# Order of work in a two-layer transformer kernel: routing, expert tiles, shared expert and norms at other places

## The chip, the cores and the metric

The kernel runs as one program on one core of a Trainium2 chip. The core has TensorE (PE, whose weight loads are shown apart as PEld), VectorE (DVE), ScalarE (ACT), GpSimd (POOL), and SyncE (SP), which here only issues DMAs. Every engine takes its own instructions in order. The metric is device time in microseconds: the median of the runs. Beside it stands one execution under the profiler, with its own time.

## The reference, cut to what matters

The input x has 8 sequences of 256 tokens with 128 channels, 2048 tokens in all. All is float32.

```python
xn = layernorm(x)
x  = x + attn0(xn) + ffn0(xn)
xn = layernorm(x)
x  = x + attn1(xn) + ffn1(xn)
# attn0: 16 heads of 8 channels, softmax over all 256 keys, output projection with bias
# ffn0:  8 experts (2 x 176 up, silu(gate)*up, 176 down); the two best of softmax(x @ gate_w.T),
#        weighted by their softmax values; plus sigmoid(x @ sg.T) * shared expert (352 wide)
# attn1: 8 query heads of 128 over one key/value head, causal, sine positions added to q and k
# ffn1:  8 experts (512 wide, gelu, biases b1 and b2); the best one of
#        softmax((x @ wg_red.T) @ unit_rows(wg).T), times its softmax value
```

Layernorm has no weights: (x - mean) / sqrt(var + 1e-5).

## The kernel before, in words

Tokens lie in 16 tiles of 128 on the partitions. `acc` (128 x 16 x 128) holds the running sum x, and every part of a layer is added into it. `xT` holds the normalised tokens, transposed. `layernorm(layer, blk)` works on blocks of four tiles: statistics on DVE (L237, L238), the square root on ACT (L240), its reciprocal and the normalised `xn` on DVE (L242, L246), four transposes on PE (L254), a copy to `xT` (L255), and a DMA of `xn` to DRAM (`xd`, L256), from which experts gather their tokens.

**Layer 0.** After four norms, the values (L448) and the router's softmax (`l0_router`), `l0_project(0)` makes queries and keys of two sequences (L466). Then the first scores of sequence 0 are computed for their maxima (L623, reduced by DVE at L638). The main loop has 64 steps, eight for each of the 8 sequences. A step computes two heads' scores of the next sequence for the maxima (L623, L638) and the same heads' scores of this one with the maxima already added (L666), which ACT turns into exponentials (L678); every second step multiplies these with the values (L693), normalises (L707 to L710) and, once a sequence, projects (L722) and adds to `acc` (L726). The scores use two PSUM tiles of two banks each (`big`); everything else has three single banks (`bank`) and one `held`.

At the end of each step `between(step)` puts in other work. In steps 0 to 10 it takes two pieces a step from `routing("l0")`, a generator: it ranks the tokens of each expert and makes the list of tokens for 40 expert tiles of 128 places (L306 to L413; the list comes from matmuls of comparison masks, L400). When it is exhausted, the first gather of tokens (`slot_tokens`, an indirect DMA on POOL, L417) and the first nine tiles' weights (`l0_weights`, on SP) are issued. From step 11 (`FIRST`) on, each step has one expert tile: its tokens are turned (`l0_turn`, L528, L530), then up matmuls (L536), silu as tanh on ACT (L544) with two DVE operations (L545, L547), then, a step later, down matmuls (L555), a copy (L564), the next weights, and after each four tiles a store of the results to DRAM (`put_results`, L435). After the last tile `l0_back` gathers the results of eight token tiles, two gathers each, and from step 59 (`COMBINE`) on `l0_combine` adds them, weighted, to one tile of `acc` a step (L579), and issues the gathers for a tile eight further.

After the loop a section works block by block: the shared expert (`shared_up`, L781, with ACT's Silu at L789 and a product at L790; `shared_down`, L797, added to `acc` at L807), the remaining sums of L579, the second `layernorm`, and layer 1's values and router logits (L847). Then follow the router (`l1_router`), the whole of `routing("l1")` for 24 expert tiles, and the biases of each tile's expert (`l1_biases`, L887 to L898).

**Layer 1.** `l1_project` (L991) makes queries and keys of two sequences at a time. Each sequence has four units (`l1_probs`, `l1_pv`): scores (L1016), the mask (L1024), maximum (L1026), exponentials with their sums (L1032), division (L1043), transposes (L1052), the product with the values (L1059) and, after four units, the projection (L1070) with one more small matmul for the experts' bias b2 weighted by the router (L1077; its operand is turned in `l1_scores_down`, L872, L880). The exponentials of a unit and the products of the one before it stand next to each other. After four sequences come the 24 expert tiles in six groups (`l1_group`: L916, L936, Gelu L945, L923, copy L956, store L435), with a ring of five weight slots filled by SP (L907, L908); then the results are gathered and added in the last two sequences (L1121).

What sets the order: the program's text gives each instruction a priority, and the tile framework's planner places instructions on each engine by its own estimate of when they are ready. So an instruction can run earlier than its place in the text: the first operation of `l1_gate_weights` (L814) stands after the loop in the text and runs at 14.17 us. Once placed, an engine's order is fixed, and an instruction that waits holds all behind it.

Of the kernel before, what the change touches and what calls it, by code (L numbers as in the profile page):

```python
# [10 lines left out]
F32 = mybir.dt.float32  # L11
# [5 lines left out]
P = 128  # L17
# [8 lines left out]
NG = 4  # L26
# [17 lines left out]
YT = 8  # L44
EPS_LN = 1e-5
# [5 lines left out]
def two_layer_kernel(  # L51
# [56 lines left out]
    eps_ln = ctile([P, 1], "eps_ln")  # L108
    nc.gpsimd.memset(eps_ln, EPS_LN)
# [72 lines left out]
    b2_s = ctile([NE, E], "b2_s")  # L182
# [7 lines left out]
    nc.gpsimd.dma_start(b2_s, b2)  # L190
# [23 lines left out]
    wqp = ctile([P, H0, ROW], "wqp", wp)  # L214
    wkp = ctile([P, H0, ROW], "wkp", wp)
# [15 lines left out]
    def layernorm(layer, blk):  # L231
# [7 lines left out]
        sd = small.tile([P, TPB], F32, tag="ln_sd", name=f"sd_{nm}")  # L239
        nc.scalar.activation(sd, mv[:, :, 1], AF.Sqrt, bias=eps_ln)  # L240
        rs = small.tile([P, TPB], F32, tag="ln_rs", name=f"rs_{nm}")
        nc.vector.reciprocal(rs, sd)  # L242
# [247 lines left out]

    ws0 = ctile([P, NTILE], "ws0")
# [30 lines left out]

    def l0_turn(i):
        g, t = divmod(i, GRP)
        if t == 0 and g + 1 < NS0 // GRP:
            xs0[g + 1] = slot_tokens(0, g + 1, r0)
        ps = bank(f"xg0_{i}")
        nc.tensor.transpose(ps[:, :P], xs0[g][:, t, :], ident)  # L528
        xg0[i] = work.tile([P, P], F32, tag="wtT", name=f"xg0_{i}")
        nc.scalar.copy(xg0[i], ps[:, :P])  # L530

    def l0_up(i):

        ps = bank(f"u0_{i}")
        for c in range(4):
# [8 lines left out]
        nc.scalar.activation(sg, ps[:IC, : 2 * P], AF.Tanh, scale=0.5)  # L544
        nc.vector.scalar_tensor_tensor(sg, sg, 1.0, ps[:IC, : 2 * P], ALU.add, ALU.mult)  # L545
        h0[i] = work.tile([IC, 2, P], F32, tag="h1", name=f"h0_{i}", bufs=3)
        nc.vector.scalar_tensor_tensor(  # L547
            h0[i].rearrange("p c n -> p (c n)"), sg, 0.5, ps[:IC, 2 * P :], ALU.mult, ALU.mult
# [36 lines left out]
    FIRST = 11  # L585
    COMBINE = FIRST + NS0 + 8

    def between(step):

        if step < FIRST:  # L590
            for _ in range(2):
                if next(routing0, routing0) is not routing0:
                    continue
                if not xs0:
                    xs0[0] = slot_tokens(0, 0, r0)
                    for i in range(RING0):
                        l0_weights(i)
        i = step - FIRST
# [9 lines left out]
        if step >= COMBINE and step - COMBINE < NTILE:  # L608
            l0_combine(step - COMBINE)
# [120 lines left out]
    for i in range(0, NI, 2):  # L730
        pair = [big_tile(f"s1_0_{i + h}") for h in range(2)]
        issue(*(max_scores(0, i + h, pair[h]) for h in range(2)))
        for h in range(2):
            max_rows(0, i + h, pair[h])

# [40 lines left out]
    def shared_up(blk):  # L776
        h = work.tile([P, len(CH), BLK], F32, tag="c", name=f"hs_{blk}")
        for c, n in enumerate(CH):
            ps = big_tile(f"sh_{blk}_{c}")
            for k in range(2):  # L780
                nc.tensor.matmul(  # L781
                    ps[:n, ts(k, BLK)],
                    lhsT=shu_s[:, k, ds(P * c, n)],
                    rhs=xT[:, ts(blk, BLK)],
                    start=True,
                    stop=True,
                )
            sg = work.tile([P, BLK], F32, tag="e", name=f"sg_{blk}_{c}", bufs=4)
            nc.scalar.activation(sg[:n, :], ps[:n, :BLK], AF.Silu)  # L789
            nc.vector.tensor_tensor(h[:n, c, :], ps[:n, BLK:], sg[:n, :], ALU.mult)  # L790
        return h

    def shared_down(blk, h):
        ps = bank(f"ds_{blk}")
        for t in range(TPB):
            for c, n in enumerate(CH):
                nc.tensor.matmul(  # L797
                    ps[:, ts(t, P)],
                    lhsT=h[:n, c, ts(t, P)],
                    rhs=shd_s[:n, c, :],  # L800
                    start=(c == 0),
                    stop=(c == len(CH) - 1),
                )
        for t in range(TPB):
            n = blk * TPB + t
            a = acc[:, n, :]
            nc.vector.scalar_tensor_tensor(  # L807
                a, ps[:, ts(t, P)], ws0[:, n : n + 1], a, ALU.mult, ALU.add
            )


    def l1_gate_weights():
        sq = small.tile([NE, 16], F32, tag="wg_sq", name="wg_sq")
        nc.vector.tensor_tensor(sq, wg_s, wg_s, ALU.mult)  # L814
        n2 = small.tile([NE, 1], F32, tag="wg_n2", name="wg_n2")
        nc.vector.tensor_reduce(n2, sq, AX.X, ALU.add)
        n1 = small.tile([NE, 1], F32, tag="wg_n1", name="wg_n1")
        nc.scalar.activation(n1, n2, AF.Sqrt)
        nc.vector.tensor_scalar_max(n1, n1, EPS_WG)
        rn = small.tile([NE, 1], F32, tag="wg_rn", name="wg_rn")  # L820
        nc.vector.reciprocal(rn, n1)
        unit = small.tile([NE, 16], F32, tag="wg_u", name="wg_u")
        nc.vector.tensor_scalar(unit, wg_s, rn, None, ALU.mult)
        ps = bank("wgT")
        nc.tensor.matmul(
            ps[:16, :NE], lhsT=unit, rhs=ident[:NE, :NE], start=True, stop=True
        )
        unitT = small.tile([16, NE], F32, tag="wg_uT", name="wg_uT")
        nc.vector.tensor_copy(unitT, ps[:16, :NE])
# [132 lines left out]
    for blk in range(NBLK + 1):  # L962
        h = shared_up(blk) if blk < NBLK else None
        if blk > 0:
            shared_down(blk - 1, late)
            for t in range((blk - 1) * TPB, blk * TPB):
                if t >= 2 * NI * NG - COMBINE:
                    l0_combine(t)
# [247 lines left out]
```

## Time and profile before

| | |
|---|---|
| runs | 674.85, 679.87, 681.44 us; median 679.87 |
| profiled execution | 677.03 us, of which the span of instructions is 675.3 |
| busy PE, PEld, DVE, ACT, POOL | 562.2, 391.7, 399.7, 261.5, 127.2 us |
| mean granted TensorE clock | 0.919 of full |
| instructions | 10890 |
| DMA | 42.20 MB, mean 62 GB/s |

Times count from the first instruction. In a timeline line the columns are start, duration (of a run of equal instructions: to its end), engine, line, operation, output <- inputs, count, and in brackets the idle time before it with what ended it. "issue" is time that an engine spent on no wait the profile shows. Busy time of PE is modelled and overlaps, so 90% busy is not 90% of what PE could do. The granted clock tells which share of full speed PE's clock had.

### The profile page before, as it was taken

To read this page: it belongs to the slowest core of one execution; us is meant where nothing else is said; L and a number is where in the kernel's file an instruction comes from. 1 tells how busy PE (TensorE), PEld (TensorE's weight loads), DVE (VectorE), ACT (ScalarE), POOL (GpSimd) and SP (SyncE) were. 2 spreads that over 40 slices of the span, in tenths; PEclk is the share of its full clock that TensorE was granted. 3 is DMA by queue.
4 is the path that set the end of the run, shared out by engine and by line. 5 is a ranking of instruction groups with operands and counts; after the bars stand their busy time and mean duration, and the time that the engine had idled before them with its cause. 6 is when DMAs were issued, how large, how long until landed. Compare 5 with 4: busy or idle time off the path is not lost.

```text
span 675.3 us, 10890 instructions
## 1 busy us (share of the span) xinstructions
PE 562.2 (83%) x3860; PEld 391.7 (58%) x3860; DVE 399.7 (59%) x942; ACT 261.5 (39%) x667; POOL 127.2 (19%) x157
## 2 busy tenths in 40 slices
PE   3879799999999998489862688897899989589786
PEld 2544566576757775145452555565668987456564
DVE  6575786667666776425647585667573324376753
ACT  2302134444544444143511024415339994141532
POOL 7100015033213201760300130000013304400000
PEclk9977799999999999799976598898899999699799
DMA  8100313144424510110100510000008972100000
GB/s 229 36 1 0 107 48 96 55 113 121 116 54 120 91 32 22 51 48 1 45 26 16 159 27 1 2 0 1 0 14 255 235 232 60 51 9 7 2 8 9
DMA packets 49863, 42.20 MB, mean 62 GB/s; under 512 B 4728, under 2 KB 44736, under 8 KB 49808
## 3 DMA queue, kind: packets, MB, share of 16 engines
q1 hardware_dynamic: 45248, 33.52, 17.2%
q0 software_dynamic: 3984, 7.71, 5.3%
q8 instruction: 31, 0.51, 0.3%
q10 hardware_dynamic: 576, 0.27, 0.2%
q14 instruction: 24, 0.20, 0.1%
HBM read 34.14 MB, written 7.34 MB: 61 GB/s over the span
## 4 chain that ended last, share of the span: by engine, by line
PE 57%; issue 16%; DVE 12%; ACT 7%; DMA 5%; POOL 1%; SPq 0%; POOLq 0%; DVEq 0%; ACTq 0%
PE s L1016 6%; PE s L623 6%; PE o L1059 5%; PE u L536 4%; PE qk L991 4%; PE wo L1070 4%; PE d L555 3%; ACT p L1032 3%; PE pv L693 3%; PE pT L1052 3%; PE d L923 2%; PE u L936 2%; PE qk L466 2%; PE s L666 2%; PE sh L781 2%
## 5 line engine op out<-in xcount | busy, mean ns | idle before, releaser
L417 POOL DMA_INDIRECT xs<-xd,d_ids_l x64 | 63.9, 999 | 342.7 <-DVE d_ids_l L413 121.9
L678 ACT ACTIVATE eT<-s 128x1024 f32<-128x1024 f32 x64 | 65.2, 1024 | 113.8 <-PE s L666 113.8
L623 PE MATMUL s<-qk 32*128 32x256 f32 x512 | 81.2, 443 | 23.0 <-DVE mx L638 22.8
L638 DVE TENSOR_REDUCE mx<-s 128x4 f32<-128x1024 f32 x64 | 77.6, 1218 | 23.4 <-PE s L666 17.0
L1016 PE MATMUL s<-kT,qT 128*128 128x128 f32 (+1 forms) x256 | 58.8, 364 | 22.5 <-ACT p L1032 22.5
L623 PEld LDWEIGHTS s<-qk 32*128 32x128 f32 x512 | 48.0, 204 | 47.5 <-DVE mx L638 30.0
L666 PE MATMUL s<-qa,qk 32*128 32x256 f32 x512 | 72.8, 416 | 2.2 <-ACT eT L678 1.2
L1032 ACT ACTIVATE p<-s,ms 128x128 f32<-128x128 f32 (+1 forms) x128 | 52.2, 428 | 41.4 <-PE s L1016 33.7
L417 POOL DMA_INDIRECT yt<-yg,d_pos_l x48 | 48.1, 1001 | 105.8 <-issue 46.9
L1016 PEld LDWEIGHTS s<-kT,qT 128*128 128x128 f32 x256 | 41.8, 206 | 37.9 <-ACT p L1032 30.6
L1059 PE MATMUL o<-pT,v 128*128 128x512 f32 x96 | 50.2, 634 | 8.3 <-DVE ms L1028 4.8
L1062 ACT COPY oT<-o 128x512 f32<-128x512 f32 x32 | 18.9, 590 | 82.3 <-PE o L1059 82.3
L666 PEld LDWEIGHTS s<-qa,qk 32*128 32x128 f32 x512 | 43.8, 192 | 8.4 <-issue 3.5
L693 PE MATMUL pv<-eT,va 128*32 128x256 f32 x512 | 42.0, 401 | 1.2 <-ACT eT L678 1.2
L536 PE MATMUL u<-xg,gu_s 128*88 128x128 f32 x320 | 41.6, 273 | 0.0
L536 PEld LDWEIGHTS u<-xg,gu_s 128*88 128x88 f32 x320 | 37.0, 157 | 0.3 <-issue 0.3
L1070 PEld LDWEIGHTS wo<-wo_s,oT 128*128 128x128 f32 x256 | 32.0, 195 | 5.2 <-issue 4.2
L1052 PE MATMUL pT<-ident,p 128*128 128x128 f32 x192 | 32.6, 312 | 2.3 <-DVE p L1043 1.3
L1070 PE MATMUL wo<-wo_s,oT 128*128 128x128 f32 x256 | 34.1, 282 | 0.0
L1043 DVE TENSOR_SCALAR p<-p,rec 128x128 f32<-128x128 f32 (+1 forms) x128 | 32.5, 317 | 1.0
L1024 DVE TENSOR_TENSOR s<-s,mask 128x512 f32<-128x512 f32 x32 | 22.3, 696 | 18.2 <-PE s L1016 18.1
L1052 PEld LDWEIGHTS pT<-ident,p 128*128 128x128 f32 x192 | 27.6, 164 | 9.1 <-DVE p L1043 2.9
(219 smaller groups left out, 945.0 us busy)
## 6 DMA issues: line engine op xcount, KB each, us to landing
w_up<-in_w_dram SPq DMA_DIRECT2D x30, 256.0 KB
gu_s<-in_gu_dram SPq DMA_DIRECT2D x40, 176.0 KB
w_down<-in_w_dram SPq DMA_DIRECT2D x18, 256.0 KB
yg<-ys SPq DMA_DIRECT2D x16, 256.0 KB
dn_s<-in_dn_dram SPq DMA_DIRECT2D x40, 88.0 KB
xd<-xn SPq DMA_DIRECT2D x8, 256.0 KB
acc<-in_x_dram SPq DMA_DIRECT2D x4, 256.0 KB
xs<-xd,d_ids_l POOLq DMA_INDIRECT x64, 2.9
```

The source lines that it names most:

```text
L417: nc.gpsimd.indirect_dma_start(out=dst, out_offset=None, in_=table, in_offset=bass.IndirectOffsetOnAxis(ap=index, axis=0), bounds_check=ta ...
L536: nc.tensor.matmul(ps[:IC, ts(c, P)], lhsT=gu0_s[:, i % RING0, c, :], rhs=xg0.get(i), start=True, stop=True,)
L623: nc.tensor.matmul(pv[:, jj, t, :], lhsT=qT[r : r + ROW, g, ds(o + t * P, P)], rhs=kT[r : r + ROW, g, ds(o, S)], start=True, stop=True,)
L638: nc.vector.tensor_reduce(m[:, ds(2 * half, 2), :, D0 + g], pv, AX.X, ALU.max, negate=True)
L666: nc.tensor.matmul(pv[:, jj, c, :], lhsT=kT[r : r + ROW, g, ds(o + c * P, P)], rhs=qa[r : r + ROW, g, :], start=True, stop=True,)
L678: nc.scalar.activation(eT.rearrange("p j c q -> p (j c q)"), ps, AF.Exp, scale=SC0)
L693: nc.tensor.matmul(po[ds(ROW * j, ROW), ts(g % 2, S)], lhsT=va_flat[:, ds(o, ROW)], rhs=eTs[j // 2][:, j % 2, c, :], start=(c == 0), stop= ...
L1016: nc.tensor.matmul(sc[:, hh, :], lhsT=qT[:, 4 * hg + hh, ds(o + t * P, P)], rhs=kT[:, ds(o, nk)], start=True, stop=True,)
L1032: nc.scalar.activation(p[:, hh, :], sc[:, hh, :], AF.Exp, bias=ms[:, hh : hh + 1], scale=SC1, accum_out=sums[:, hh : hh + 1],)
L1052: nc.tensor.transpose(ps[:, ts(hh, P)], p[:, hh, ts(c, P)], ident)
L1059: nc.tensor.matmul(po, lhsT=v1[:, 2 * b + c, :], rhs=pT[:, c, :], start=(c == 0), stop=(c == t))
L1070: nc.tensor.matmul(ps[:, ts(t, P)], lhsT=oT[:, h, ts(t, P)], rhs=wo1_s[:, h, :], start=(h == 0), stop=False,)
```

## The change

1. `routing("l0")` is taken in pieces between the four pairs of first scores (five pieces a pair), and its rest before the loop; there the first gather, the first nine tiles' weights and the first turn are issued too. Tiles begin at step 3 (`TILES`) in place of 11. (`between` calls the turn of tile 0 in step 2 once more, with its gather of the second group.)
2. The shared expert goes into steps 44 to 59, three steps of `shared_up` (one chunk each, two single banks in place of a big tile, tanh and two DVE operations in place of Silu and one) and one of `shared_down` per block.
3. The sums of L579 go two tiles a step into steps 50 to 57.
4. The second norms of blocks 0, 1, 2 go into steps 53, 55, 59, and layer 1's first projection into steps 56 to 63; only the last norm, the values and the router follow the loop.
5. `routing("l1")` is taken one piece per unit of layer 1's attention; the first gather, first weights and biases are issued when it is exhausted.
6. 1/sqrt in `layernorm` is an add and a power (-0.5) on POOL, in place of ACT's square root and DVE's reciprocal.
7. b2 is no longer added by matmuls in the projection. Each expert tile's weights bring a third DMA, its b2 row broadcast to all partitions (`bias2`), and DVE adds it when it empties the down matmuls' bank (one per tile, in place of one copy per group from `held`). The router's weighted one-hots and their transposes go, and the score is a maximum.
8. `l1_gate_weights` stands before layer 0's router in the text.

```diff
+TILES = 3
+SHARED = TILES + NS0 + 1
+COMBINE = SHARED + 6
+NORM1 = (COMBINE + 3, COMBINE + 5, COMBINE + 9)
+PROJECT1 = COMBINE + 6
...
-        nc.scalar.activation(sd, mv[:, :, 1], AF.Sqrt, bias=eps_ln)
         rs = small.tile([P, TPB], F32, tag="ln_rs", name=f"rs_{nm}")
-        nc.vector.reciprocal(rs, sd)
+        nc.gpsimd.tensor_scalar_add(rs, mv[:, :, 1], EPS_LN)
+        nc.gpsimd.tensor_tensor(rs, rs, minus_half, ALU.pow)
...
+    def silu_times(dst, half, g, u):
+        nc.scalar.activation(half, g, AF.Tanh, scale=0.5)
+        nc.vector.scalar_tensor_tensor(half, half, 1.0, g, ALU.add, ALU.mult)
+        nc.vector.scalar_tensor_tensor(dst, half, 0.5, u, ALU.mult, ALU.mult)
...
     def between(step):
-        if step < FIRST:
-            for _ in range(2):
-                if next(routing0, routing0) is not routing0:
-                    continue
...
-        i = step - FIRST
+        i = step - TILES
...
-        if step >= COMBINE and step - COMBINE < NTILE:
-            l0_combine(step - COMBINE)
+        blk, c = divmod(step - SHARED, len(CH) + 1)
+        if 0 <= blk < NBLK:
+            if c < len(CH):
+                shared_up(blk, c)
+            else:
+                shared_down(blk)
+        if 0 <= step - COMBINE < NTILE // 2:
+            for t in range(2):
+                l0_combine(2 * (step - COMBINE) + t)
+        if step in NORM1:
+            layernorm(1, NORM1.index(step))
+        if step >= PROJECT1:
+            for _ in range(2):
+                next(project1, None)
...
             max_rows(0, i + h, pair[h])
+        for _ in range(5):
+            next(routing0, None)
+    for _ in routing0:
+        pass
+    xs0[0] = slot_tokens(0, 0, r0)
+    for i in range(RING0):
+        l0_weights(i)
+    l0_turn(0)
...
+        nc.sync.dma_start(
+            bias2[:, i % len(ring), :],
+            b2[ds(r, 1), :].rearrange("e c -> (e c)").partition_broadcast(P),
+        )
...
+            nc.vector.tensor_tensor(ys[:, t, :], pd[:, :P], bias2[:, n, :], ALU.add)
             l1_weights(g * GRP + t + len(ring))
...
+    layernorm(1, NBLK - 1)
+    for blk in range(NBLK):
+        l1_values(blk)
     oh1 = l1_router()
     r1 = Routing()
-    for _ in routing("l1", [oh1], NS1, r1):
-        pass
-    own_b1 = l1_biases(r1.expert)
+    routing1 = routing("l1", [oh1], NS1, r1)
...
                 late = (b, hg, t, p, oT)
+                if not ahead and next(routing1, routing1) is routing1:
+                    ahead.append(slot_tokens(1, 0, r1))
+                    for i in range(len(ring)):
+                        l1_weights(i)
+                    own_b1 = l1_biases(r1.expert)
```

## The prediction

> **What bounds the kernel now.** I cut the span into stages (view of busy time by stretch) at events of the timeline: first scores at 36.4, the first expert tile's matmuls (L536) at 105.1, the last tile's (L555) at 263.7, layer 1's first scores (L1016) at 395.8. Columns: start and end, length, then busy time and count on PE, PEld, DVE, ACT, POOL, then granted clock, DMA share, GB/s.
>
> ```profile
> 36.00:51.00 15.00, 10.93 (x66) 6.76 (x64) 10.84 (x19) 0.69 (x1) 0.00 (x0) 0.68 0.00 1
> 51.00:98.00 47.00, 41.61 (x302) 25.96 (x300) 33.70 (x79) 11.97 (x13) 0.21 (x1) 0.81 0.19 53
> 98.00:264.00 166.00, 159.70 (x1615) 111.54 (x1612) 113.22 (x181) 76.73 (x170) 39.78 (x40) 1.00 0.32 82
> 264.00:302.00 38.00, 23.40 (x234) 11.61 (x232) 14.15 (x27) 11.59 (x14) 25.99 (x26) 0.87 0.19 51
> 302.00:362.00 60.00, 44.17 (x208) 27.92 (x207) 32.92 (x121) 19.31 (x28) 6.11 (x6) 0.92 0.09 26
> 362.00:386.00 24.00, 11.45 (x46) 9.93 (x45) 15.78 (x62) 0.97 (x2) 0.20 (x1) 0.50 0.39 110
> 396.00:503.00 107.00, 92.82 (x432) 63.38 (x433) 71.25 (x168) 40.32 (x151) 0.18 (x1) 0.94 0.01 1
> 503.00:561.00 58.00, 54.61 (x447) 52.11 (x447) 18.76 (x37) 53.89 (x138) 15.76 (x16) 1.00 0.76 214
> ```
>
> PE sets the pace where the tiles run (159.7 of 166 us at full clock). From 264 to 386 nothing is full: PE is busy 79 of 122 us, and from 362 at half clock. The timeline shows why:
>
> ```profile
> 270.36 0.35 DVE L579 SCALAR_TENSOR_TENSOR acc<-yt,wr,acc 128x128 f32<-128x128 f32 x1 [2.31 <-DMA yt<-yg,d_pos_l]
> 275.89 0.79 PE L623 MATMUL s<-qk 32*128 32x256 f32 x2 [7.31 <-DVE mx L638]
> 320.67 1.28 ACT L240 ACT_TABLE_LOAD   x1
> 376.04 3.58 PE L400 MATMUL ids_l<-col_l,row_l 128*128 128x24 f32 x16 [7.02 <-DVE col_l L395]
> ```
>
> The sums L579 stand ahead of the maxima L638 in DVE's order and wait for gathers that Pool issues every 1.30 us, so PE waits 7.3 us. Later norms and shared expert alternate through table loads, and layer 1's routing leaves PE idle.
>
> **The change, stage by stage.** The sum is made on the profiled execution: 677.03 us, a span of 675.3 and 1.7 around it; the median of 679.87 is 2.8 above.
>
> *To 36.4: 0 (-1 to +4).* No row shows Pool's add and power on 128x4. Near rows: 0.09 us (memset 128x1), 0.14 (iota 128x16), 1.26 (tensor add 128x512). I take 0.25 each, near the small ones, against 0.30 on ACT and 0.18 on DVE now. Pool is busy with DMA issues and memsets until 11.15, so the first normalising xn goes from 9.37 to about 11.3; behind it on Pool stand the bias adds (1.26), for which DVE doesn't wait. The third block's xn already waits for the store of xn until 17.33, which covers this; without that cover it costs 2. The gate weights' square already runs at 14.17, so moving its code up is nothing.
>
> *36.4 to the first tile: -23 (-30 to -17).* Now 68.7 us. Routing costs DVE 18.8 us (59 instructions, 65.2 to 97.5) and PE eight groups of ids matmuls, 1.98 us each at full clock. The first scores use DVE for 8 x 1.22 of their 13.4 us. With both together from 39.18, ids are ready at 39.2 + 9.8 + 18.8 = 67.7 at the earliest; from ids to the first tile it is 7.8 (97.3 to 105.1: four gathers, landing, transpose), where steps 0 to 2 and the second projection fit: 75.5. The other end: eight steps fewer stand ahead of the tile, each 2.46 us without extra work (265.71 to 268.17): 105.1 - 19.7 = 85.4. I take 82, nearer to the second, since the second projection's 7 to 9 us of PE and three steps need room too. Beside it the clock: granted 0.68 there, and a group of ids matmuls takes 3.58 at 0.50. The Trainium skill (TensorE: Matmul & The Clock Gate, Part 1) says that the clock is halved after an idle window of about 3.4 us and released by sustained work. By that rule, were PE mostly waiting for DVE here, the eight groups would cost 28.6 instead of 15.8 us, and the tile would start near 88 if nothing covered it. The 0.50 row agrees with the rule.
>
> *Tiles: 0 (0 to +2).* 41 steps in 158.6 us, PE full, whatever their numbers. The first turn is called twice (ahead of the loop and in step 2): four gathers (5.2 us of Pool, busy 40 of 166), a transpose of 0.27, a copy of 0.25.
>
> *Last tile to layer 1's first scores: -32 (-42 to -6).* Now 132.2 us. What PE must do there: 12 steps of 1.9 (a batch of eight takes 28.85 with tiles at 1.7 a step) = 22.8; 8 steps without maxima of 1.65 (1.13 + 0.53) = 13.2; shared up 48 x 0.43 = 20.6; shared down 4 x 2.7 = 10.8; transposes 4 x 1.1; projection 18 x 0.43 = 7.7; values 4 x 2.2 = 8.8. Together 88. At the tiles' idle share (4%) that is 91, at that of 264 to 362 (67.6 of 98 busy) 128. I take 100, nearer to the first, since score work now stands between the shared expert's. What keeps it from 91: DVE has about 70 us here (12 x 1.22 maxima, 24 x 0.69 for silu, which is 8.3 more than with one product, 32 x 0.30 sums, 16 x 0.28, norms 3 x 3, projection 9 x 0.75, transposes). A shared chunk holds two of the three banks through two matmul pairs, tanh 0.60 and two DVE operations of 0.69, about 3.9 us, or 5.1 with a maximum between. Seven table loads go (three of L240, three of L789, one of L266), 7 x 1.28 = 9.0 us of ACT, inside this stage. The Trainium skill (ScalarE: Activation LUTs, What ACT_TABLE_LOAD costs) adds 1.38 us of drain to each, so by it 18.6 us would go. Here the activation begins at 321.96, right after the load of 320.67: no drain is seen, and 9.0 stands. Routing of layer 1 (24 us from 362) leaves this stage.
>
> *Layer 1, first half: +5 (-3 to +15).* Routing goes between 12 units of attention: 10.7 us of DVE and four groups of matmuls (7.2 at half clock, 3.6 at full), where DVE is busy 71 of 107 and PE 93. The biases' 3.7 of DVE follow. If gaps took it all it would be 0; I take a third. SP can issue the first five expert weights when the experts are known, a batch or more ahead of their use.
>
> *Experts and rest: 0 (-4 to +8).* A bias row is 128 packets more. Queue 1's 45248 packets took 17.2% of 16 x 675 us, 41 ns each: 0.33 us over 16 engines, 19 refills 6 us. The refill fills DMA for half of the stage:
>
> ```profile
> 515.00:530.00 15.00, 13.56 (x116) 13.11 (x114) 2.92 (x8) 14.74 (x42) 5.15 (x6) 1.00 0.92 263
> 530.00:545.00 15.00, 13.94 (x110) 12.99 (x109) 5.27 (x12) 14.82 (x38) 3.76 (x4) 1.00 1.04 264
> ```
>
> I take +4 of the 6. On SP a third issue is some 0.55 us on 1.7 per tile (373.62 to 375.32), below the stage's 2.4. DVE's 24 adds of 0.35 less 6 copies of 0.69 are 4.3, under DVE's 39 idle. Against it go the bias matmuls, 16 x 0.41, and the turned scores, 4 x 1.04 of PE; some 4 of these 11 lie on the path here and in the first half.
>
> Sum: -23 - 32 + 5 + 0 = -50, so 627 in the profile's terms. I say **628** for a median.
>
> **Rivals.** *The gathers hold the norms (648).* Pool is in order: the last sums' 16 gathers (20.8 us) can stand ahead of a norm's power, and DVE's xn, with the maxima behind it, waits. For: 264 to 288 lost 14 us over four steps (23.6 against 9.8). Against: seven steps of about 4 now lie between the tiles and the sums. Price: the 20.8 once, 627 + 21.
>
> *More is hidden (605).* Stage 2 at 75.5 and the fourth at 91 give 677 - 30 - 42. For: the tile stage shows that PE can be filled. Against: three banks and DVE.
>
> *Order isn't made by the program (675).* Instructions are placed by a planner: the gate's square is program-late and runs at 14.17. If the moves left the order as it is, only bias matmuls and loads count, within 1%. Against: the shared matmuls begin only at 302, behind the last scores.
>
> *Slower: one row of biases holds the experts (760).* All rows lie in one tile. If the add of a tile waited for the row last asked for, each tile would take that DMA's time; 7.55 us lies on the chain behind full queues:
>
> ```profile
> 535.78 7.55 DMA w_down<-in_w_dram
> ```
>
> 24 x (7.55 + 0.35 - 2.4) = 132 more, 759. It decides from 4.5 us a tile (2.4 + 50/24). Against: the weights are slots of one tile too, and PE waits only 0.5 us for them.
>
> **Chances.** Forecast (612 to 640) 0.55, more hidden 0.13, gathers 0.20, no change 0.04, slower 0.08. One per cent is about what a measurement of this kernel can tell from no change. Range 600 to 660: it takes in the fast rival and the gathers, and leaves out the last two. Faster 0.88, same 0.04, slower 0.08.
>
> **What will show it.** The first L536 near 82, the last L555 near 241, first L1016 near 341, first expert matmul (L936) near 452. No waits of maxima behind L579 above 3 us. No table load between 110 and the first L936. PE's clock above 0.9 in the norms. If L246 waits for Pool by more than 5 us, the gathers' rival holds; if ids are ready only after 85, the second stage is wrong; if the expert stage is over 70 us, the bias rows. What would make it wrong most: DVE as the bound of the fourth stage.

## The result, and the profile after

The changed kernel takes **647.92 us** (median of 645.86 to 651.23, four runs) against 679.54 for the kernel before beside it: a ratio of **0.955** (0.949 to 0.961). That is faster by 31.6 us, where 50 were forecast; 648 lies inside the range of 600 to 660. In the profiled execution 29.2 us of span are gone (675.3 to 646.1). The column c1 is the profiled execution of a second comparison of the same two kernels (below).

| stage, us | before | forecast change | after | c1 |
|---|---|---|---|---|
| start to first scores | 36.4 | 0 | 38.8 | 34.9 |
| first scores to first tile | 68.7 | -23 | 58.4 | 57.8 |
| 40 expert tiles | 158.4 | 0 | 158.3 | 158.4 |
| last tile to layer 1's first scores | 132.3 | -32 | 104.6 | 106.1 |
| layer 1, first half | 107.7 | +5 | 116.6 | 118.1 |
| layer 1's experts and the rest | 171.8 | 0 | 169.4 | 168.7 |

The first stage of one and the same kernel is 34.9 in one execution and 38.8 in another, so its +2.4 can't be put down to the change. A stage is read from one profiled execution of a kernel, and among the experiments below those of e8, e9 and e10 lie 12, 10 and 9 us above the fastest run of their kernel and that of e3 lies 11 us under its median, so small differences in these four say little. The forecast's gain is missing in three stages: 13 us in the second, 4 to 6 in the fourth, 4 to 5 in the fifth. Line numbers from here on are those of the changed kernel: ids matmuls L406, gathers L423, Pool's addition and power L247 and L248, `xn` L252, projection L472, turn L565, up L572, sums L613, shared up L628, shared down L643, maxima L741, layer 1's scores L1022, its experts L979 and L965.

Busy time by stretch, after the change (columns as in the prediction: start and end, length, PE, PEld, DVE, ACT, POOL, granted clock, DMA share, GB/s):

```profile
38.80:76.00 37.20, 28.61 (x141) 22.67 (x140) 26.97 (x75) 0.69 (x1) 0.00 (x0) 0.62 0.24 66
76.00:97.10 21.10, 17.55 (x92) 8.93 (x92) 6.68 (x7) 6.24 (x9) 12.15 (x12) 0.79 0.15 38
97.10:255.50 158.40, 153.48 (x1544) 107.97 (x1541) 108.17 (x174) 73.95 (x167) 31.85 (x32) 1.00 0.33 83
255.50:360.10 104.60, 83.46 (x610) 43.91 (x608) 66.19 (x155) 28.89 (x37) 36.05 (x38) 0.93 0.12 31
```

The fourth stage before the change:

```profile
263.70:395.80 132.10, 89.13 (x509) 53.70 (x508) 69.91 (x219) 32.17 (x42) 39.97 (x40) 0.82 0.18 50
```

The ids are ready at 75.7, but the first tile starts only at 97.1. The tiles' stage is as it was. The fourth stage, before at a clock of 0.82 (0.50 from 362 to 386), now runs at 0.93, and PE is busy 80% of it instead of 67%.

What lies between the ids and the first tile, in the timeline after the change:

```profile
75.50 0.20 DVE L416 TENSOR_TENSOR d_idf_l<-ids_l,d_idf_l 128x40 f32<-128x40 f32 x1 [1.51 <-PE ids_l L406]
...
79.06 0.47 PE L565 MATMUL xg<-ident,xs 128*128 128x128 f32 x1 [3.59 <-DMA xs<-xd,d_ids_l]
...
79.75 9.63 PE L472 MATMUL qk<-xT,wqkp 128*128 128x512 f32 x16
...
89.31 1.13 PE L769 MATMUL s<-qa,qk 32*128 32x256 f32 x8
...
97.15 1.11 PE L572 MATMUL u<-xg,gu_s 128*88 128x128 f32 x8
```

PE waits 3.6 us for the first gather, because the extra turn ahead of the loop is first in its queue. Then comes the second block's projection, 9.6 us, with little beside it and half of it at a granted clock of 0.50 (79.7 to 84.5; 0.95 from there to 89.4). Then come steps 0 to 2, 7.8 us. Before the change the projection took as long, 54.0 to 63.3, also with little beside it, but ahead of the routing; its first and last rows there:

```profile
54.02 1.92 PE L466 MATMUL qk<-xT,wqp 128*128 128x512 f32 x2
...
62.30 1.02 PE L466 MATMUL qk<-xT,wkp 128*128 128x512 f32 x2
```

And the longest stop in the fourth stage:

```profile
289.76 1.00 POOL L423 DMA_INDIRECT yt<-yg,d_pos_l  x1 [0.31 <-issue]
290.79 0.26 POOL L247 TENSOR_SCALAR rs<-mv 128x4 f32<-128x4 f32 x1
291.13 1.04 POOL L248 TENSOR_TENSOR rs<-rs,minus_half 128x4 f32<-128x4 f32 x1
292.21 0.60 DVE L252 TENSOR_SCALAR xn<-acc,mv,rs 128x128 f32<-128x128 f32 x2 [5.99 <-POOL rs L248]
...
293.46 2.02 PE L628 MATMUL sh<-xT,shu_s 128*96 128x512 f32 x2 [10.49 <-DVE sg L557]
```

Pool has issued 24 gathers since 259.74, one each 1.30 us, and only then comes to the addition and the power of the first norm. DVE stands at `xn` for 6.0 us (after two waits of 2.3 for sums), and behind `xn` in DVE's order stands the silu product that would free a bank for PE: PE loses 10.5 us at one wait.

### The profile page after: what moved, and what is told of

Its sections match the earlier page's. It is cut to its first block, busy times and chain, and to the rows that moved or that the text cites. A ratio compares the mean times of both kernels' runs of the same rounds, so it can differ in the third digit from the quotient of the medians.

```text
span 646.1 us, 10887 instructions
## 1 busy us (share of the span) xinstructions
PE 543.4 (84%) x3797; PEld 380.6 (59%) x3797; DVE 400.6 (62%) x959; ACT 245.1 (38%) x649; POOL 140.9 (22%) x176
## 4 chain that ended last, share of the span: by engine, by line
PE 53%; DVE 14%; issue 14%; DMA 8%; POOL 6%; ACT 5%; POOLq 0%; SPq 0%; DVEq 0%; ACTq 0%
PE s L726 6%; PE s L1022 5%; PE u L572 5%; PE o L1065 5%; PE qk L668 4%; PE qk L472 4%; PE d L589 3%; PE pv L796 3%; POOL yt L423 3%; PE pT L1058 3%; PE wo L1076 3%; ACT p L1038 3%; PE s L769 3%; PE d L965 2%; DMA yt<-yg,d_pos_l 2%
## 5 line engine op out<-in xcount | busy, mean ns | idle before, releaser
L423 POOL DMA_INDIRECT xs<-xd,d_ids_l x68 | 68.1, 1001 | 279.4 <-DVE d_ids_l L419 126.2
L741 DVE TENSOR_REDUCE mx<-s 128x4 f32<-128x1024 f32 x64 | 77.9, 1218 | 18.4 <-PE s L769 12.4
L726 PE MATMUL s<-qk 32*128 32x256 f32 x512 | 78.2, 419 | 12.7 <-DVE mx L741 12.5
L1022 PE MATMUL s<-kT,qT 128*128 128x128 f32 (+1 forms) x256 | 57.7, 362 | 20.2 <-ACT p L1038 20.2
L769 PE MATMUL s<-qa,qk 32*128 32x256 f32 x512 | 71.5, 401 | 1.1 <-DVE qa L752 0.7
L726 PEld LDWEIGHTS s<-qk 32*128 32x128 f32 x512 | 46.4, 192 | 36.0 <-DVE mx L741 20.6
L423 POOL DMA_INDIRECT yt<-yg,d_pos_l x48 | 48.1, 1002 | 79.2 <-issue 46.5
L1022 PEld LDWEIGHTS s<-kT,qT 128*128 128x128 f32 x256 | 42.1, 209 | 33.5 <-ACT p L1038 27.2
L572 PE MATMUL u<-xg,gu_s 128*88 128x128 f32 x320 | 41.6, 273 | 0.0
L796 PE MATMUL pv<-eT,va 128*32 128x256 f32 x512 | 37.3, 391 | 0.6 <-ACT eT L781 0.6
L572 PEld LDWEIGHTS u<-xg,gu_s 128*88 128x88 f32 x320 | 37.0, 157 | 0.3 <-issue 0.3
L628 PE MATMUL sh<-xT,shu_s 128*128 128x512 f32 (+1 forms) x48 | 26.8, 673 | 10.5 <-DVE sg L557 10.5
L988 ACT ACTIVATE h<-u,own_b 128x128 f32<-128x128 f32 x96 | 26.4, 379 | 20.5 <-PE u L979 20.4
L472 PE MATMUL qk<-xT,wqkp 128*128 128x512 f32 x64 | 33.6, 679 | 0.0
```

The lines of the kernel that those rows point to most:

```text
L423: nc.gpsimd.indirect_dma_start(out=dst, out_offset=None, in_=table, in_offset=bass.IndirectOffsetOnAxis(ap=index, axis=0), bounds_check=ta ...
L472: nc.tensor.matmul(ps, lhsT=w[:, ts(g, 4), :], rhs=xT[:, ts(blk, BLK)], start=True, stop=True,)
L572: nc.tensor.matmul(ps[:IC, ts(c, P)], lhsT=gu0_s[:, i % RING0, c, :], rhs=xg0.get(i), start=True, stop=True,)
L726: nc.tensor.matmul(pv[:, jj, t, :], lhsT=qT[r : r + ROW, g, ds(o + t * P, P)], rhs=kT[r : r + ROW, g, ds(o, S)], start=True, stop=True,)
L741: nc.vector.tensor_reduce(m[:, ds(2 * half, 2), :, D0 + g], pv, AX.X, ALU.max, negate=True)
L769: nc.tensor.matmul(pv[:, jj, c, :], lhsT=kT[r : r + ROW, g, ds(o + c * P, P)], rhs=qa[r : r + ROW, g, :], start=True, stop=True,)
```

## The experiments

Each comparison runs kernels and the kernel before on one chip. In the comparison of e5 to e7 and c1 the kernel before takes 677.9 us; with e1 to e4, e8 to e10 and e11 it takes 720 to 722. It isn't the chip: one chip gave 677.9 with e5 and 722.0 with e11. So ratios are compared within a level, and stages too. The changed kernel itself ran at the level of 678 only.

| stage, us | e1 | e2 | e3 | e4 | e8 | e9 | e10 | e11 | c1 | e5 | e6 | e7 |
|---|---|---|---|---|---|---|---|---|---|---|---|---|
| level of before | 720 | 720 | 720 | 720 | 720 | 720 | 720 | 722 | 678 | 678 | 678 | 678 |
| to first scores | 33.1 | 33.9 | 36.2 | 40.1 | 38.2 | 40.3 | 39.7 | 40.0 | 34.9 | 33.3 | 33.6 | 38.5 |
| to first tile | 56.1 | 55.0 | 58.0 | 57.1 | 58.3 | 54.4 | 54.4 | 54.3 | 57.8 | 53.0 | 58.3 | 58.3 |
| tiles | 165.9 | 165.8 | 165.8 | 165.9 | 167.3 | 167.8 | 167.8 | 165.9 | 158.4 | 158.4 | 158.4 | 158.4 |
| to layer 1's scores | 117.8 | 113.7 | 115.1 | 113.7 | 175.2 | 115.1 | 113.4 | 114.3 | 106.1 | 106.0 | 106.6 | 104.7 |
| first half | 118.8 | 117.1 | 111.8 | 116.2 | 102.8 | 118.9 | 119.9 | 114.8 | 118.1 | 116.5 | 123.1 | 120.2 |
| experts and rest | 173.1 | 173.1 | 176.1 | 174.6 | 175.4 | 174.8 | 175.7 | 178.7 | 168.7 | 169.5 | 172.1 | 169.3 |
| ratio | 0.928 | 0.924 | 0.939 | 0.929 | 0.991 | 0.927 | 0.926 | 0.928 | 0.952 | 0.955 | 0.970 | 0.964 |

### c1, the changed kernel again

> The changed kernel once more, on the chip of the three runs sent with it, so that their stages can be set against its own. Measured first: ratio 0.955 to before (0.949 to 0.961); stages 38.8, 58.4, 158.3, 104.6, 116.6, 169.4. If the chip is one on which before takes 720 us, the ratio should be the same, so 687 us; if it lies near 0.93 instead, the first turn and the 1/sqrt that the first four runs took away were worth nothing.

Measured: 646.10 us, ratio 0.952 (0.947 to 0.957); stages as in the first table. So the result is repeatable, and the stop of 10.49 us at L628 is there again with 10.5.

### e1, without the first turn ahead of the loop

```diff
         l0_weights(i)
-    l0_turn(0)
```

> The changed kernel without the first turn ahead of the loop; it stays in step 2 alone. Theory (the turn holds TensorE's queue): in the changed kernel TensorE waits 3.59 us for the first gather in L565, with the mask transposes and the second projection (16 matmuls, 9.6 us at half clock) behind it. Without it these start about 75.5 instead of 79.1, so the first tile goes from 97.1 to 93 or 94, and the time from 648 to about 644. Rival (the steps and the projection set the tile's start, and the gathers a wait that only moves): first tile within 1 us of 97.1, time within 1 us.

Measured: the stage is 56.1, against 58.0 and 57.1 in e3 and e4, which have the turn at the same level; ratio 0.928 (0.923 to 0.933). Of the ids' 21 us to the first tile 17.7 are left. The wait for the gather is gone and the projection starts at 70.08, beside the last ids, but three steps and most of the projection still stand ahead of the tile. The ids come 1.4 us later than in e3 and e4 (38.4 after the first scores, against 36.9 and 37.0). So the turn cost 1 to 2 us, and the larger part was what stood behind it: theory and rival each had a part.

### e2, the projection written behind the first scores

```diff
+    qa0 = l0_augment(0)
+    l0_project(1)
     for _ in routing0:
         pass
...
-    l0_turn(0)
...
```

> As the run before, and in addition the mask transposes and the second block's projection are written ahead of the last part of the routing. Theory (TensorE is idle and cold beside the routing, 28.6 of 37.2 us busy at half clock up to 76, and then does 9.6 us of projection with nothing beside it): the projection fits beside the routing, the first tile goes to 97.1 - 3.6 - 9.6 = 84, time 635 to 638. Rival (VectorE is what the routing waits for): its 4 additions of 0.75 and the 1.22 of qa delay the ids from 75.7 to 80, first tile 88 to 89, time 639 to 641. No gain at all would say that the clock or the tile's weights hold the tile.

Measured: ratio 0.924 (0.918 to 0.929), the stage 55.0. This edit didn't put the projection beside the routing: five pieces a pair use up the routing's pieces within the four pairs of first scores, so nothing of it was left behind them, and the projection ran from 70.9 to 80.5, behind the last ids matmuls. The run says only that the place behind the routing is worth 1 us. The question itself is e5's.

### e5, the projection among the first scores

```diff
             max_rows(0, i + h, pair[h])
+        if i == 2:
+            l0_project(1)
         for _ in range(5):
             next(routing0, None)
...
-    l0_turn(0)
...
-        if b % 2 == 0 and b + 2 < B:
+        if b % 2 == 0 and 0 < b and b + 2 < B:
             l0_project(b // 2 + 1)
```

> The changed kernel without the first turn ahead of the loop, and with the second block's projection written among the first scores, ahead of the routing's second group of steps. Theory (the projection is 9.6 us of matmuls that came beside the routing before the change and after it since): the stretch from the ids to the first tile goes from 21.4 to about 10 (three steps of 2.5, and the gather beside them), the ids come at most 2 us later; time 10 to 12 us less than the control, ratio about 0.938 where the control has 0.955. Rival (routing and projection need the same three banks and the same VectorE): ids 6 to 9 us later, first tile within 4 us of the control's, time 0 to 4 us less.

Measured: the ids come 40.9 after the first scores (c1: 37.0), the first tile 12.1 after the ids (c1: 20.8); the stage is 4.8 shorter, 53.0. PE in the timeline of e5:

```profile
48.58 1.05 PE L406 MATMUL ids_l<-col_l,row_l 128*128 128x40 f32 x8 [1.40 <-DVE col_l L401]
...
54.14 1.93 PE L406 MATMUL ids_l<-col_l,row_l 128*128 128x40 f32 x8
...
72.38 0.67 PE L750 MATMUL mT<-ident,mx 128*128 128x128 f32 x2
...
86.31 0.89 PE L572 MATMUL u<-xg,gu_s 128*88 128x128 f32 x6
```

Directly behind the projection a group of ids takes 1.05 us, later, when PE has gaps again, 1.93. So the projection did fit among the routing, at a price of 3.9 us for the ids: about half of what theory gave, between it and the rival. Part of the gain was lost behind the ids. With no projection there, the three steps ran at a granted clock of 0.53, though the records show PE busy throughout; in the changed kernel they took 7.8 us at 1.00:

```profile
74.40:86.30 11.90, 11.90 (x73) 6.88 (x73) 2.45 (x2) 3.23 (x4) 8.17 (x8) 0.53 0.17 44
```

The median is 644.6, ratio 0.955 (0.948 to 0.961): from the control's 646.1 this can't be told apart.

### e3 and e4, 1/sqrt on ScalarE and on VectorE

e3, as before the change:

```diff
-        nc.gpsimd.tensor_scalar_add(rs, mv[:, :, 1], EPS_LN)
-        nc.gpsimd.tensor_tensor(rs, rs, minus_half, ALU.pow)
+        nc.scalar.activation(sd, mv[:, :, 1], AF.Sqrt, bias=eps_ln)
+        nc.vector.reciprocal(rs, sd)
```

> The changed kernel with 1/sqrt as before the change: square root on ScalarE, reciprocal on VectorE. Theory (Pool's gathers hold the norms): TensorE's wait of 10.5 us at 283 and VectorE's 8.7 us for rs go, two table loads of 1.28 a norm come back on ScalarE, which is busy only 29 of the 105 us; the stage from the last tile to layer 1's first scores goes from 104.6 to between 94 and 100, the first scores from 38.8 back to 36.5, time 638 to 643. Rival (the sums wait for the gathers' data in any case, so VectorE stands as long): stage 104 to 112 with the loads, time 648 to 655.

e4, by Newton steps from a first guess on the bits:

```diff
-        nc.gpsimd.tensor_scalar_add(rs, mv[:, :, 1], EPS_LN)
-        nc.gpsimd.tensor_tensor(rs, rs, minus_half, ALU.pow)
+        nc.vector.tensor_scalar_add(va, mv[:, :, 1], EPS_LN)
+        nc.vector.tensor_scalar(rs.bitcast(I32), va.bitcast(I32), 1, None, ALU.arith_shift_right)
+        nc.vector.tensor_scalar(rs.bitcast(I32), rs.bitcast(I32), -1, 0x5F3759DF, ALU.mult, ALU.add)
+        for _ in range(3):
+            nc.vector.tensor_tensor(nw, rs, rs, ALU.mult)
+            nc.vector.scalar_tensor_tensor(nw, nw, -0.5, va, ALU.mult, ALU.mult)
+            nc.vector.scalar_tensor_tensor(rs, nw, 1.5, rs, ALU.add, ALU.mult)
```

> The changed kernel with 1/sqrt of the norms on VectorE: a shift and a subtraction on the bits for a first guess, then three Newton steps, 12 instructions on 128x4 in place of Pool's two; 12 x 0.16 = 1.9 us of VectorE a norm (estimated from 128x16 instructions of 0.17 us). Theory (Pool's gathers hold the norms): no wait for rs, stage from the last tile to layer 1's first scores 92 to 97 instead of 104.6, time 637 to 642. Rival (VectorE is the bound of that stage): 3 x 1.9 = 5.7 us more there, and the waits move to the sums: stage 104 to 110, time 648 to 654.

Measured: e3 0.939 (0.935 to 0.944; five runs from 664.7 to 678.6, median 675.5, the profiled one the lowest), e4 0.929 (0.923 to 0.935; median 670.1); the stage 115.1 and 113.7, where Pool's form gives 117.8 (e1) and 113.7 (e2) at the same level. So in the profiled executions the place of 1/sqrt moves the stage by no more than e1 and e2 differ with the same form. By the medians ScalarE's form is 5 us slower than VectorE's, with ranges that overlap; where these lie, the profile of e3, its lowest run, doesn't show. The 12 small instructions of e4 take 2.1 us a norm. The table loads that e3 brings back cost 1.28 us each on ScalarE:

```profile
304.57 1.28 ACT L248 ACT_TABLE_LOAD   x1
305.87 0.30 ACT L248 ACTIVATE sd<-mv,eps_ln 128x4 f32<-128x4 f32 x1
```

Why there is little to gain at this level is seen in e2's timeline, in the first group of the shared expert's down matmuls beside the gathers. First the same 24 matmuls in the changed kernel's own profile, then e2's first rows with Pool's:

```profile
267.74 2.94 PE L643 MATMUL ds<-shd_s,hs 128*128 128x128 f32 x24
```

```profile
267.44 0.39 PE L643 MATMUL ds<-shd_s,hs 128*128 128x128 f32 x2 [0.49 <-issue]
...
268.01 1.00 POOL L423 DMA_INDIRECT yt<-yg,d_pos_l  x1 [0.30 <-issue]
268.15 0.27 PE L643 MATMUL ds<-shd_s,hs 128*128 128x128 f32 x1 [0.32 <-issue]
...
268.87 0.99 PE L643 MATMUL ds<-shd_s,hs 128*128 128x128 f32 x4 [0.45 <-issue]
269.31 1.00 POOL L423 DMA_INDIRECT yt<-yg,d_pos_l  x1 [0.30 <-issue]
...
280.26 1.23 DVE L741 TENSOR_REDUCE mx<-s 128x4 f32<-128x1024 f32 x1 [12.57 <-PE ds L643]
```

The matmuls last to 278.9, 11.5 us in place of 2.9, and come by threes and fours while Pool issues a gather each 1.30 us; DVE waits 12.6 us. In the changed kernel's own profile Pool issues the same gathers at the same pace, and these matmuls don't stop. The same level shows it in the tiles: 165.9 in place of 158.4, with eight waits of about 2 us in e4 (DVE's silu, "issue"), each beside one of the eight groups of four gathers. So at this level other engines slow down beside gathers, whatever stands behind these in Pool's queue. And the stop that e3 and e4 were to remove is small here: PE's wait for the silu product behind `xn`, 10.5 us in the changed kernel's profile, is 2.6 in e1, with Pool's form. What makes the level isn't known.

### e9 and e11, e5 with the Newton steps

> The second projection among the first scores, no first turn ahead of the loop, and the norms' 1/sqrt by Newton steps on VectorE. Theory (24 gathers ahead of the first norm in Pool's queue cost TensorE 10.5 us at one wait): the stage from the last tile to layer 1's first scores goes from 106 to 95 to 99, ratio 0.937 to 0.943 where the projection alone gave 0.955 (0.948 to 0.961). Rival (VectorE, or the sums' own wait for gathers, holds that stage anyway, as the second chip's 113.7 by either way suggests): stage 103 to 107, ratio 0.950 to 0.956.

> The kernel of e9 once more. The chips of this study are of two kinds: on two of them the kernel before takes 678 to 680 us, on two 720, where engines stand for 12 to 17 us while Pool issues gathers, and where the norms' place made no difference. If this run falls on the first kind: theory (gathers ahead of the first norm in Pool's queue) stage from the last tile to layer 1's first scores 95 to 99 instead of 106.0, no wait for 10.5 us of the shared expert's matmuls, time 634 to 640; rival (VectorE or the sums' own wait holds the stage) 103 to 107, time 643 to 648. If it falls on the second kind: stage 113 to 116 and ratio 0.927 as in e9, and the question stays open.

Both fell on the level of 720: ratios 0.927 (0.922 to 0.932) and 0.928 (0.923 to 0.932), the stage 115.1 and 114.3. The wait for `rs` is gone, but at this level it was small (6.4 us in all in e1 and in e2), and the Newton steps of three norms take about as much on DVE. The longest wait in the stage is the one of this level, and e1 has it too, with Pool's form (waits by engine, e11 and e1; "remote" is a release the profile doesn't place):

```profile
DVE mx L752 <- remote: 13.5, 1, 13.5
```

```profile
DVE mx L741 <- PE ds L643: 13.5, 1, 13.5
```

What e11's expectation says of two kinds of chips is wrong: its chip had been at the other level before. At the level of 678, where the stop of 10.5 us stands behind Pool's queue, neither form ran, so their worth there stays **open**.

### e8, the order undone

```diff
-        blk, c = divmod(step - SHARED, len(CH) + 1)
-        if 0 <= blk < NBLK:
-            ...
-        if step in NORM1:
-            layernorm(1, NORM1.index(step))
-        if step >= PROJECT1:
-            ...
+        if step >= COMBINE and step - COMBINE < NTILE:
+            l0_combine(step - COMBINE)
...
+    for blk in range(NBLK + 1):
+        ...
```

> The changed kernel with the shared expert, the last sums, the norms, and the projections of layer 1 written behind layer 0's attention again, in the order of before; the tanh form of silu and Pool's 1/sqrt stay, so no table loads come back. Theory (the 28 us of the stage from the last tile to layer 1's first scores come from filling TensorE there): that stage goes from 105 or 106 back to 122 to 132 (132.1 before the change, up to 9 of which were table loads), time 663 to 671, ratio 0.978 to 0.99. Rival (the table loads and the serial norms were what cost): stage under 112, ratio under 0.965.

Measured: 716.1 us, ratio 0.991 (0.986 to 0.995); the stage is 175.2, against 113 to 118 in every other kernel of that level, and the first half 102.8 in place of 112 to 120. Waits in that stage of e8 (its L610 are the sums, L711 and L726 first scores and maxima, L735 the maxima's transposes, L249 and L257 `xn` and its transposes):

```profile
PE mT L735 <- DVE mx L726: 25.3, 2, 24.7
...
PE lnT L257 <- DVE xn L249: 18.4, 4, 5.8
...
DVE acc L610 <- DMA yt<-yg,d_pos_l: 17.8, 15, 2.2
DVE mx L726 <- remote: 17.4, 1, 17.4
PE s L711 <- DVE mx L726: 16.7, 7, 7.4
```

Two kinds of stop of the kernel before are among them, maxima behind sums (7.4 us the longest) and serial norms (18.4 us in four waits), and no table load is. The longest, 24.7, is for the most part the halt of this level: DVE stands 17.4 us of it at a maximum while Pool issues gathers, as it stands 12.6 to 13.5 in e1 and e2 with the new order, so 4 to 5 us of the difference may be the halt's. The rest is the order's. So it is the order that carries the fourth stage at this level; e8 undoes shared expert, sums, norms and projections together, and which of them carries how much isn't shown. Its size at this level (57 to 62 us in the stage, 41 to 51 with the first half, 48 in the medians against e1's 668.3) isn't the size at 678, where the whole stage lost 26 to 28.

### e6, the biases by matmul

```diff
-            nc.vector.tensor_tensor(ys[:, t, :], pd[:, :P], bias2[:, n, :], ALU.add)
...
+            nc.tensor.matmul(
+                ps[:, ts(t, P)],
+                lhsT=wtT[b // 2][:, ts(2 * (b % 2) + t, P)],
+                rhs=b2_s,
+                start=False,
+                stop=True,
+            )
...
```

> The changed kernel with the second biases as before the change: turned scores, and a matmul of 8 rows a tile pair in layer 1's output projection, no bias rows by DMA. Theory (rows cost the experts' stage 4 of the 6 us of their DMA time; the matmuls and turned scores cost 11 us of TensorE, about half on the path): experts' stage from 63 to 58 or 59, the rest 5 to 8 longer, time 1 to 4 us more than the control. Rival (the rows hold the experts): the experts' stage goes below 57 and the time is 3 us or more under the control's.

Measured: 656.56, ratio 0.970 (0.966 to 0.974), 10.5 us over the control. The expert stretch alone:

```profile
480.00:536.20 56.20, 52.29 (x428) 49.89 (x428) 16.81 (x32) 52.14 (x135) 15.30 (x16) 1.00 0.80 221
```

```profile
475.30:537.50 62.20, 53.88 (x435) 50.79 (x435) 21.93 (x58) 47.04 (x132) 15.16 (x16) 1.00 0.83 220
```

The first is e6, the second the control: the rows, with their additions and a bank for each tile, cost 6.0 us there. Little of this is waiting for DMA: in the control PE waits 2.1 us for weights, 3.9 for turned tokens (`xgT`, copied on DVE) and 2.3 for Gelu's result, in e6 1.5, 1.9 and 0.3. Everything after it is 9.4 shorter with rows (106.5 against 115.9), and the first half 5.0 (118.1 against 123.1). So the biases are a gain of 8 us in these stages, more than theory had, and of the other sign than the rival.

### e7, layer 1's routing written whole ahead of its attention

```diff
-    routing1 = routing("l1", [oh1], NS1, r1)
+    for _ in routing("l1", [oh1], NS1, r1):
+        pass
+    own_b1 = l1_biases(r1.expert)
...
```

> The changed kernel with layer 1's routing written whole ahead of layer 1's attention, as before the change. Theory (spread between the attention's units, the routing costs 9 us of the first half instead of 24 with TensorE waiting): first scores of layer 1 20 to 25 us later than the control's, the first half 9 us shorter (107.5 before the change), time 11 to 16 us more. Rival (the planner lays attention beside the routing anyway, as it lays the first scores beside the ids): time within 3 us of the control's.

Measured: 652.39, ratio 0.964 (0.960 to 0.968). Layer 1's first scores come as before (stage 104.7), the ids at 399.4 instead of 440.9, and the first half is 120.2 against 116.6 and 118.1. The planner lays attention beside the routing from whichever place, as the rival said; but its time, within 3 us of the control's, was missed: writing the routing in pieces is worth 2 to 4 us by this stage, 6 by the medians.

### e10, all rows of biases at once

```diff
-        nc.sync.dma_start(bias2[:, i % len(ring), :], b2[ds(r, 1), :]...)
...
+            r = nc.vector.value_load(r1.expert_i[0:1, i : i + 1], min_val=0, max_val=NE - 1)
+            row = bias2[:, ds(r, 1), :].rearrange("p o c -> p (o c)")
+            nc.vector.tensor_tensor(ys[:, t, :], pd[:, :P], row, ALU.add)
...
```

> As the run before, and the eight rows of second biases are brought once, by one DMA, ahead of layer 1's attention; the addition of a tile takes its row by the expert's number, read into a register on VectorE. Theory (the rows cost the experts' stage 6.0 us, 62.2 against 56.2, as DMA time beside the weights): that stage 56 to 58, time 4 to 6 us under the run before. Rival (it is the additions and their banks, not the DMAs): stage 61 to 63, same time. If the register reads stall VectorE by more than its idle time, the stage is longer than 63.

Measured: 0.926 (0.921 to 0.931) beside e9's 0.927. The expert stretch is 61.0 in e10, 63.7 in e9 and 65.7 in e11, the stretch behind it 114.7 against 111.1 and 113.0: nothing is won in all. The stretch fits the rival (61 to 63); since e9 and e11, one kernel, differ by 2.0, the DMAs' part can't be told closer than 3 to 5 us. No version here beats the changed kernel by more than the comparisons can tell.

## Why the prediction was right, and where not

The side and the range held; the likeliest time was 20 us too low. By the stages of the profiled execution: 2.4 of these are the start, 12.7 the second stage, 4.3 the fourth, 3.9 the fifth, and the last gives 2.4 back.

**36.4 to the first tile: wrong.** The step that failed is "from ids to the first tile it is 7.8", "where steps 0 to 2 and the second projection fit". They don't: after the change it is 21.4, of which the gather with the early turn ahead of it takes 3.6, the projection 9.6 and the three steps 7.8. Before the change the projection took its 9.3 us ahead of the routing; the bound of 75.5 has no place for it, and the 6.5 us between 75.5 and 82 were too few for the "7 to 9 us of PE and three steps" named there. The ids were ready 36.9 us after the first scores, in place of 31.3 by the bound (67.7 less 36.4). So the tile came 19.3 us later than the bound, 13.6 of it behind the ids and 5.6 ahead of them, where 6.5 were allowed. The other end, 85.4, has the projection in it, but takes the routing to be shorter by the whole length of eight steps, 19.7. Between first scores and ids, without the projection, the change won 14.7 (51.6 to 36.9), and 3.6 of it went to the early turn.

The sign given for this stage, ids only after 85, didn't show: they were ready at 75.7. No run undoes the earlier tiles alone, so their gain of 10 to 11 us is read from the stages only.

A second error lay in a row: 1.98 us (16 instructions) is two groups of ids matmuls, not one. Eight groups are 8 us at full clock and 15 at half, so the price given for a cold clock, 13 us, was twice too high. The groups did run cold: 1.93 each at a granted clock of 0.62 in the stretch, 1.05 in e5 right behind dense matmuls. The Trainium skill (TensorE: Matmul & The Clock Gate, Part 1) has the clock halved when PE idles and restored by sustained work. The 0.56 in c1's routing, and e5's 0.72 with the projection in it, go that way. e5's 0.53 behind the ids, with PE busy throughout by the records, does not, and no run here tells why.

**Tiles: right**, 158.3.

**Last tile to layer 1's first scores: right in kind.** The forecast was 100, measured 104.6 and 106.1. That order is the cause is shown by e8, at the other level; at 678 the order was not undone. The sum of PE's work held (83.5 busy, 88 counted). What was mis-sized is the share of stops: the gathers' stop of 10.5 was held for a rival. Without it the stage would be near 94 to 96, by subtraction, nearer to the end of 91; no run shows it.

**The gathers' rival** was given 20.8 once and 0.20. By the prediction's own mark, `xn` waiting for Pool by more than 5 us, it holds in part: 8.7 us of waits for `rs` in this stage, 6.0 the longest, at a price of 10.5. The time came out at its 648 by chance: two thirds of the missing 20 us lie in the second stage. "DVE as the bound of the fourth stage" was not what failed: DVE is busy 66 of 105.

**Table loads.** None is left between the tiles and the experts, as forecast. What the 9.0 us of ScalarE are worth on the path isn't settled: e8 has none of the loads and still shows the long stage, so they are not its cause, but e3, which brings six back in the stage, is 5 us slower than e4 by the medians. Among the experts, loads stay: 12 in c1's stretch of 62.2, as exponentials of the attention stand between the Gelus there.

**Layer 1's first half: +9 to +10, not +5.** The step that failed is "I take a third": that gaps would take two thirds of the routing. With the bias matmuls put back (e6) the half is 123.1, 15.4 over the kernel before, and the routing with the first biases was priced at 18 to 22 us of DVE and PE, so most of it lies on the path. The biases' part there is a gain of 5.0 (e6).

**Experts: +6.0 for the rows, where 4 were taken.** That the size came near is in part luck: the forecast counted DMA time alone, and most of what PE waits longer than in e6 is not for DMA. The removed matmuls and turns are worth 14.4 where 4 of 11 were taken, so the stage came out at -2 to -3, where 0 was forecast. The rival of 760 needed a row's DMA in each tile's path; the stage is 62 to 63, under its mark of 70.

**Pool's 1/sqrt:** the addition is 0.26 where 0.25 was taken, the power 1.04 instead of 0.25. At the start its effect can't be seen, since the first stage differs by 4 us between executions of one kernel.

## What to carry to other kernels

When a piece of work is moved ahead, list what it is moved past, on each engine, and ask whether that still stands in the way: here a projection of 9.3 us ahead of the routing became one of 9.6 behind it, and the forecast of the tile had given it too little room. Don't put a short operation that others wait for into the queue of an engine that issues long rows of DMAs; its own time (1.3 us) is not its price (10.5). Order can be worth more where stops are long: undone at the level where engines slow down beside gathers, it cost 57 to 62 us in a stage that the whole change shortened by 26 to 28 at the other level.

## What the runs showed of the hardware that was not expected

- Pool's power on 128x4 takes 1.04 us, its addition on 128x4 0.26.
- In e5, PE ran the three steps behind the ids at a granted clock of 0.53 while the records show it busy for 11.9 of 11.9 us.
- At the level of 720 us for the kernel before, with the same instructions at the same lengths, PE, DVE and ACT halt or creep while Pool issues gathers: 24 matmuls in 11.5 us instead of 2.9, the tiles' stage 7.5 us longer with eight waits of 2 us, DVE standing 12.6 to 17.4 us at one maximum in e1, e2 and e8. One chip showed both levels. That the gathers take part is argued from where the stops stand; no run is without gathers, and what sets the level was not tried.
- An estimate of the change at that level: e1 lacks only the turn, which is worth 1 to 2 us, so about 670 against 720, a gain of 7% where it is 4.5 to 4.8% at the other.
